# Layer norms of a graph network with the features on partitions, their product on GpSimd

## The chip, the cores and the metric

One core of a Trainium2 chip (trn2). The metric is the device time of one execution in microseconds. Each kernel ran several times; medians of all runs are quoted. All runs of this study are of the fast state. Ratios are computed as the mean time of one kernel's fast runs over that of the other's of the same rounds, so they are not quite the ratio of the medians quoted beside them.

## The reference

Sixteen graphs of 1024 nodes and 128 features share one sparse adjacency matrix (some 8 neighbours a node). Four layers follow each other: attention, graph attention (GAT), attention, attention. Only the end of each layer matters here:

```python
# attention layers (L0, L2, L3)
x1 = layer_norm(x + attn @ Wo + bo, ln1_g, ln1_b)
x  = layer_norm(x1 + relu(x1 @ W1 + b1) @ W2 + b2, ln2_g, ln2_b)
# graph attention layer (L1)
x  = layer_norm(x + attn, ln_gamma, ln_beta)

def layer_norm(x, g, b):       # over the 128 features
    mu, var = x.mean(-1, keepdims=True), x.var(-1, keepdims=True)
    return (x - mu) * rsqrt(var + 1e-5) * g + b
```

## The kernel before

The work is cut into 64 units (layer, half of the graphs, tile of 128 nodes) and each unit into parts. For each part GpSimd issues gathers of neighbour rows, VectorE makes the products, ScalarE the exponentials, TensorE the sums. What follows the sums of a unit, its **tail**, runs in two halves of four graphs each, interleaved with the next unit's parts: a tail is a generator, and `others()` advances all tails by about one step at each of three places in a part. Each engine works through its own instructions in program order; the timelines below show later ones waiting behind earlier ones.

```python
STEPS = 15            # steps of an attention unit's tails, spread evenly over the unit
GRAPH_STEPS = 8
...
def normed(y):                                   # y: nodes on partitions, PSUM
    z = twos.tile([P, GH, D], F32, tag="o", name="z")
    total = smalls.tile([P, GH], F32, tag="total", name="total")
    for i in range(GH):                          # GH = 4 graphs
        nc.scalar.activation(z[:, i, :], y[:, i, :], AF.Square, scale=D**-0.5, bias=root,
                             accum_out=total[:, i : i + 1])
    yield
    rstd = smalls.tile([P, GH], F32, tag="rstd", name="rstd")
    nc.gpsimd.tensor_tensor(rstd, total, power, ALU.pow)
    yield
    for i in range(GH):
        nc.scalar.activation(z[:, i, :], y[:, i, :], AF.Copy, scale=rstd[:, i : i + 1])
    return z

def turned(z, dst, gain=None, shift=None):       # transposes, then the eviction
    ps = bank([P, GH, P])
    for i in range(GH):
        nc.tensor.transpose(ps[:, i, :], z[:, i, :], ident)
    ...
        nc.scalar.activation(dst, ps, AF.Identity, bias=shift, scale=gain)

def attention_tail(l, g, t, h, o):
    ...
    for i in range(GH):                          # Wo, and x less its mean
        nc.tensor.matmul(ps[:, i, :], oT[:, i, :], p["Wo"], start=True, stop=False)
        nc.tensor.matmul(ps[:, i, :], xt[:, i, :], centre, start=False, stop=True)
    yield
    z = yield from normed(ps)
    yield
    x1 = twos.tile([P, GH, P], F32, tag="oT", name="x1")
    turned(z, x1, p["ln1_g"], p["ln1_b"])
    yield
    ...                                          # W1 and ReLU, then W2 + centre into ps
    z = yield from normed(ps)
    yield
    yield from finish(l, g, t, h, z, p["ln2_g"], p["ln2_b"])    # turned, next layer's projection

# the loop over parts, cut
    products(i)                                  # VectorE
    summed(i - 2)                                # TensorE
    others()
    exponentials(i)                              # VectorE reduce, ScalarE Exp
    others()
    weighted(i - 1, 0)                           # VectorE; frees the buffer of part i-1
    gathered(i - 1 + AHEAD)                      # GpSimd; waits for that buffer
    others()
```

Of the kernel before, what the change touches and what calls it, by code (L numbers as in the profile page):

```python
# [11 lines left out]

F32 = mybir.dt.float32
BF16 = mybir.dt.bfloat16
I32 = mybir.dt.int32
AF = mybir.ActivationFunctionType
ALU = mybir.AluOpType
# [3 lines left out]
P = 128  # L21
D = 128
# [3 lines left out]
F = FF // P  # L26
EPS = 1e-5
# [18 lines left out]
GH = G // HF  # L46
# [65 lines left out]
AHEAD = 4  # L112

LIMIT = 1e25


def rows_of(v, n=P):
# [5 lines left out]
def sparse_path(ctx: ExitStack, tc: tile.TileContext, a: dict, out: bass.AP, flag):  # L123


    nc = tc.nc
    const = ctx.enter_context(tc.tile_pool(name="const", bufs=1))
    dram = ctx.enter_context(tc.tile_pool(name="dram", bufs=1, space=DRAM))
    banks = ctx.enter_context(tc.tile_pool(name="banks", bufs=4, space=PSUM))
    ybanks = ctx.enter_context(tc.tile_pool(name="ybanks", bufs=2, space=PSUM))  # L130
    accs = ctx.enter_context(tc.tile_pool(name="accs", bufs=1, space=PSUM))

    def bank(shape):
        return banks.tile(shape, F32, tag="ps", name="ps")

    ident = const.tile([P, P], F32, name="ident")
    make_identity(nc, ident)

    centre = const.tile([P, P], F32, name="centre")
# [11 lines left out]
        q = slice(0, P) if whole else slice(32 * j, 32 * j + 32)  # L151
        return rep[q, j].rearrange("p s n -> p (s n)")

    power = const.tile([P, GH], F32, name="power")
    nc.vector.memset(power, -0.5)

    root = const.tile([P, 1], F32, name="root")
    nc.vector.memset(root, (EPS / D) ** 0.5)


    idx = const.tile([P, 2, T, J, QUADS], I32, name="idx")
# [8 lines left out]
    wts = ctx.enter_context(tc.tile_pool(name="wts", bufs=2))  # L170
    states = ctx.enter_context(tc.tile_pool(name="states", bufs=2))
# [4 lines left out]
    twos = ctx.enter_context(tc.tile_pool(name="twos", bufs=2))  # L176
# [260 lines left out]
    w = {}  # L437
# [12 lines left out]
    def load_weights(layer):  # L450



        t = wts.tile([P, 2 * D], F32, tag="Wkv", name="Wkv")
        nc.sync.dma_start(t[:, :D], a[f"{layer}_gnn_Wk"])
        nc.sync.dma_start(t[:, D:], a[f"{layer}_gnn_Wv"])
        w[layer, "Wkv"] = t
        yield
        for name in ATTN:
            src = a[f"{layer}_gnn_{name}"]  # L460
            if name in ("Wq", "Wo", "W1"):
                t = wts.tile([P, src.shape[1]], F32, tag=name, name=name)
                nc.sync.dma_start(t, src)
            elif name == "W2":
                t = wts.tile([P, F, D], F32, tag=name, name=name)
                nc.sync.dma_start(t, src.rearrange("(f p) d -> p f d", p=P))
            elif name == "b1":
                t = wts.tile([P, F], F32, tag=name, name=name)
                with nc.allow_non_contiguous_dma(reason="a bias, once"):
                    nc.sync.dma_start(t, src.rearrange("(f p) -> p f", p=P))  # L470
            elif name.startswith("ln") or name in ("b2", "bo"):
                t = wts.tile([P, 1], F32, tag=name, name=name)
                nc.sync.dma_start(t, src.rearrange("(p o) -> p o", o=1))
            else:
                continue
            w[layer, name] = t
        yield
        centred(w[layer, "Wo"], D)
        centred(w[layer, "W2"].rearrange("p f d -> p (f d)"), F * D)
        ps = bank([P, F])  # L480
        for f in range(F):
            nc.tensor.matmul(
                ps[:, f : f + 1], w[layer, "W1"][:, f * P : (f + 1) * P], w[layer, "b2"],
                start=True, stop=True,
            )
        nc.vector.tensor_tensor(w[layer, "b1"], w[layer, "b1"], ps, ALU.subtract)
        nc.vector.tensor_tensor(w[layer, "ln1_b"], w[layer, "ln1_b"], w[layer, "b2"], ALU.add)

    wg = const.tile([P, D + 2], F32, name="wg")

# [32 lines left out]
    xs = {}  # L523
# [48 lines left out]
        nc.sync.dma_start(table[:, h * GH * D : (h + 1) * GH * D], kv[:, : GH * D])  # L572
        nc.sync.dma_start(table[:, ROW + h * GH : ROW + (h + 1) * GH], kv[:, GH * D :])

    def normed(y):

        z = twos.tile([P, GH, D], F32, tag="o", name="z")
        total = smalls.tile([P, GH], F32, tag="total", name="total")
        for i in range(GH):
            nc.scalar.activation(  # L580
                z[:, i, :], y[:, i, :], AF.Square, scale=D**-0.5, bias=root,
                accum_out=total[:, i : i + 1],
            )
        yield
        rstd = smalls.tile([P, GH], F32, tag="rstd", name="rstd")
        nc.gpsimd.tensor_tensor(rstd, total, power, ALU.pow)  # L586
        yield
        for i in range(GH):
            nc.scalar.activation(z[:, i, :], y[:, i, :], AF.Copy, scale=rstd[:, i : i + 1])  # L589
        return z  # L590

    def turned(z, dst, gain=None, shift=None):
# [4 lines that stand above are left out]
        if gain is None:  # L597
            nc.scalar.copy(dst, ps)  # L598
        else:
            nc.scalar.activation(dst, ps, AF.Identity, bias=shift, scale=gain)  # L600

    def over_graphs(v):
        return v.rearrange("p (o d) -> p o d", o=1).to_broadcast([P, GH, D])

    def finish(l, g, t, h, z, gain, shift):
        if l + 1 < len(LAYERS):

            wanted[0] = True
            while held[0]:
                advance(slow)  # L610
            wanted[0] = False
            busy[0] += 1
            xn = states.tile([P, GH, P], F32, tag="xT", name="xT")
            turned(z, xn, gain, shift)
            yield
            yield from project(l + 1, g, t, h, xn)
            busy[0] -= 1
            return
        xn = states.tile([P, GH, P], F32, tag="xT", name="xT")
        turned(z, xn, gain, shift)  # L620
        yield
        o = twos.tile([P, GH, D], F32, tag="kv", name="outs")
        turned(xn, o)
        yield
        nc.gpsimd.indirect_dma_start(  # L625
            out=out.rearrange("n (k c) -> (n k) c", k=GR * HF),
            out_offset=bass.IndirectOffsetOnAxis(ap=places[:, g, h, t : t + 1], axis=0),
            in_=o.rearrange("p g d -> p (g d)"), in_offset=None,
        )

    def attention_tail(l, g, t, h, o):
        layer = LAYERS[l][0]
        p = {n: w[layer, n] for n in ATTN if (layer, n) in w}
        xt = xs[l, g, t][:, h]
        for _ in range(h):
            yield
        oT = twos.tile([P, GH, P], F32, tag="oT", name="oT")
        turned(o, oT)

        nc.scalar.activation(xt, xt, AF.Identity, bias=p["bo"])  # L640
        yield
        ps = ybanks.tile([P, GH, D], F32, tag="yps", name="yps")
        for i in range(GH):
            nc.tensor.matmul(ps[:, i, :], oT[:, i, :], p["Wo"], start=True, stop=False)  # L644
            nc.tensor.matmul(ps[:, i, :], xt[:, i, :], centre, start=False, stop=True)  # L645
        yield
        z = yield from normed(ps)
        yield
        x1 = twos.tile([P, GH, P], F32, tag="oT", name="x1")
        turned(z, x1, p["ln1_g"], p["ln1_b"])  # L650
        yield
        f1 = ones_.tile([P, F, GH * P], F32, tag="f1", name="f1")
        for f in range(F):
            ps = bank([P, GH * P])
            nc.tensor.matmul(  # L655
                ps, p["W1"][:, f * P : (f + 1) * P], x1.rearrange("p g n -> p (g n)"),
                start=True, stop=True,
            )
            nc.scalar.activation(f1[:, f, :], ps, AF.Relu, bias=p["b1"][:, f : f + 1])  # L659
        yield  # L660
        ps = ybanks.tile([P, GH, D], F32, tag="yps", name="yps")
        for i in range(GH):
            for f in range(F):
                nc.tensor.matmul(  # L664
                    ps[:, i, :], f1[:, f, i * P : (i + 1) * P], p["W2"][:, f, :],
                    start=(f == 0), stop=False,
                )
            nc.tensor.matmul(ps[:, i, :], x1[:, i, :], centre, start=False, stop=True)
        yield
        z = yield from normed(ps)  # L670
        yield
        yield from finish(l, g, t, h, z, p["ln2_g"], p["ln2_b"])

    def graph_tail(l, g, t, h, o):
        for _ in range(h):
            yield
        ps = ybanks.tile([P, GH, D], F32, tag="yps", name="yps")
        nc.tensor.matmul(
            ps.rearrange("p g d -> p (g d)"), ident, o.rearrange("p g d -> p (g d)"),
            start=True, stop=False,  # L680
        )
        for i in range(GH):
            nc.tensor.matmul(  # L683
                ps[:, i, :], xs[l, g, t][:, h, i, :], centre, start=False, stop=(i == GH - 1)
            )
        yield
        z = yield from normed(ps)
        yield
        yield from finish(l, g, t, h, z, w["L1", "ln_gamma"], w["L1", "ln_beta"])

    def natural(g, t, h, rows, kv=None):
# [325 lines left out]
    with tc.manual_schedule():  # L1017
# [37 lines left out]
        for i in range(len(parts) + 2):  # L1055
            here = i < len(parts)
            u = parts[i][0] if here else len(units)
            if here:
                l = units[u][0]
# [491 lines left out]
```

## Time and profile before

| | before |
|---|---|
| time, median (range) | 2544.95 us (2538.24 to 2557.18), 4 runs |
| busy: TensorE, VectorE, ScalarE, GpSimd | 82%, 75%, 58%, 57% |
| TensorE at half rate, after the first 250 us | 62 stretches, 357 us |
| VectorE waiting for gathers' transfers | 149 us |

The prediction below shows the waits, the stretches of one unit and the rows of the normalisation. Here, for comparison with later runs, are the rows of VectorE's two large products, from the groups of instructions by form; after the bar stand busy us, the mean in ns, and the idle time ahead of them with what ended it:

```profile
L919 DVE TENSOR_TENSOR pr<-e,ex 128x2048 f32<-128x2048 f32 x264 | 601.5, 2288 | 46.6 <-ACT ex L895 22.2 <-ACT ex L907 17.6 <-PE ps L596 3.7
L868 DVE TENSOR_TENSOR pr<-e,qr 128x2048 f32<-128x2048 f32 x198 | 453.4, 2290 | 177.8 <-PE acc L935 80.7 <-DMA e<-table,idx 70.6 <-ACT qr L831 16.8
```

A product of 128x2048 takes 2.29 us here in the mean. The runs below show what a longer mean comes from.

### The profile page before, as it was taken

To read this page: it belongs to the slowest core of one execution; us is meant where nothing else is said; L and a number is where in the kernel's file an instruction comes from. 1 tells how busy PE (TensorE), PEld (TensorE's weight loads), DVE (VectorE), ACT (ScalarE), POOL (GpSimd) and SP (SyncE) were. 2 spreads that over 40 slices of the span, in tenths; PEclk is the share of its full clock that TensorE was granted. 3 is DMA by queue.
4 is the path that set the end of the run, shared out by engine and by line. 5 is a ranking of instruction groups with operands and counts; after the bars stand their busy time and mean duration, and the time that the engine had idled before them with its cause. 6 is when DMAs were issued, how large, how long until landed. Compare 5 with 4: busy or idle time off the path is not lost. (4 is left out here: it accounts for less than half of the span.)

```text
span 2561.0 us, 36646 instructions
## 1 busy us (share of the span) xinstructions
PE 2102.6 (82%) x13124; PEld 1303.1 (51%) x13124; DVE 1930.3 (75%) x1470; ACT 1474.6 (58%) x4640; POOL 1450.8 (57%) x978
## 2 busy tenths in 40 slices
PE   6558989788887888988788888988888787888786
PEld 5425656445554554554455554555555454445454
DVE  7887787587877466667887879788797877787782
ACT  3216776565665444455476656667666665566555
POOL 3334666366666588784545545455555656665652
PEclk8679999899898999999899999999999898989888
DMA  7646888667678589898777877788777667567660
GB/s 251 232 170 230 293 280 287 210 227 252 231 257 260 175 282 327 281 322 297 276 256 248 298 258 261 255 283 277 264 267 254 222 240 260 203 222 257 222 222 24
DMA packets 168461, 636.05 MB, mean 248 GB/s; under 512 B 38328, under 2 KB 41144, under 8 KB 119774
## 3 DMA queue, kind: packets, MB, share of 16 engines
q0 software_dynamic: 92672, 485.09, 54.2%
q1 hardware_dynamic: 75600, 148.55, 17.4%
q8 instruction: 105, 1.72, 0.3%
q14 instruction: 84, 0.69, 0.1%
HBM read 603.11 MB, written 92.34 MB: 272 GB/s over the span
## 5 line engine op out<-in xcount | busy, mean ns | idle before, releaser
L856 POOL DMA_INDIRECT e<-table,idx x600 | 925.7, 1543 | 455.9 <-DVE pr L919 245.6
L919 DVE TENSOR_TENSOR pr<-e,ex 128x2048 f32<-128x2048 f32 (+1 forms) x336 | 689.5, 2060 | 205.0 <-ACT ex L895 174.2
L868 DVE TENSOR_TENSOR pr<-e,qr 128x2048 f32<-128x2048 f32 x204 | 460.7, 2258 | 177.8 <-PE acc L935 80.7
L586 POOL TENSOR_TENSOR rstd<-total,power 128x4 f32<-128x4 f32 x224 | 333.1, 1490 | 392.6 <-ACT z L580 385.4
L935 PE MATMUL acc<-pr,marks 128*32 128x512 f32 x2656 | 495.1, 618 | 38.2 <-DVE pr L919 38.2
L891 DVE TENSOR_REDUCE sc<-pr 128x128 f32<-128x2048 f32 (+1 forms) x252 | 518.5, 2058 | 8.6
L580 ACT ACTIVATE z<-yps,root 128x128 f32<-128x128 f32 x896 | 318.5, 378 | 98.5 <-PE yps L683 49.8
L596 PE MATMUL ps<-ident,z 128*128 128x128 f32 x896 | 212.7, 338 | 161.8 <-ACT z L589 161.7
L589 ACT ACTIVATE z<-yps,rstd 128x128 f32<-128x128 f32 x896 | 257.3, 381 | 102.4 <-POOL rstd L586 102.3
L596 PEld LDWEIGHTS ps<-ident,z 128*128 128x128 f32 x896 | 136.0, 159 | 345.4 <-ACT z L589 251.8
L659 ACT ACTIVATE f<-ps,b 128x512 f32<-128x512 f32 x192 | 131.9, 690 | 275.8 <-PE ps L655 275.8
L655 PE MATMUL ps<-x,W 128*128 128x512 f32 x384 | 249.1, 783 | 35.9 <-ACT x L600 35.8
L664 PE MATMUL yps<-W,f 128*128 128x128 f32 x1536 | 259.7, 287 | 17.0 <-ACT f L659 15.9
L664 PEld LDWEIGHTS yps<-W,f 128*128 128x128 f32 x1536 | 212.2, 196 | 77.5 <-ACT f L659 58.6
L935 PEld LDWEIGHTS acc<-pr,marks 128*32 128x32 f32 x2656 | 102.0, 112 | 283.8 <-issue 223.9
L538 PE MATMUL ps<-Wkv,xT 128*128 128x256 f32 x768 | 208.7, 416 | 32.7 <-ACT xT L600 24.1
L831 ACT COPY qr<-ps 128x512 f32<-128x512 f32 x384 | 197.0, 600 | 61.3 <-PE ps L828 55.7
L580 ACT ACTIVATION_READ_ACCUMULATOR z<-yps,root 128x1 f32 x896 | 194.1, 217 | 0.0
L542 ACT COPY kv<-ps 128x512 f32<-128x512 f32 x176 | 103.3, 589 | 140.9 <-PE ps L538 117.1
L538 PEld LDWEIGHTS ps<-Wkv,xT 128*128 128x128 f32 x768 | 146.4, 202 | 73.1 <-ACT xT L600 30.0
L644 PE MATMUL yps<-Wo,oT 128*128 128x128 f32 x768 | 160.9, 292 | 6.0 <-ACT oT L598 6.0
L645 PE MATMUL yps<-centre,x 128*128 128x128 f32 x768 | 158.0, 288 | 6.6
(159 smaller groups left out, 2663.6 us busy)
## 6 DMA issues: line engine op xcount, KB each, us to landing
table<-kv SPq DMA_DIRECT2D x88, 512.0 KB
qx<-qr SPq DMA_DIRECT2D x96, 256.0 KB
kept<-xT SPq DMA_DIRECT2D x96, 256.0 KB
x<-kept SPq DMA_DIRECT2D x48, 512.0 KB
e<-table,idx POOLq DMA_INDIRECT x600
table<-kv SPq DMA_DIRECT2D x32, 256.0 KB
edges<-in_adj SPq DMA_DIRECT2D x8, 512.0 KB
spare<-in_x SPq DMA_DIRECT2D x8, 512.0 KB
```

The costliest lines, as they stand in the source:

```text
L538: nc.tensor.matmul(ps[:, k, :], x[:, i + k, :], w[LAYERS[l][0], "Wkv"], start=True, stop=True,)
L580: nc.scalar.activation(z[:, i, :], y[:, i, :], AF.Square, scale=D**-0.5, bias=root, accum_out=total[:, i : i + 1],)
L586: nc.gpsimd.tensor_tensor(rstd, total, power, ALU.pow)
L589: nc.scalar.activation(z[:, i, :], y[:, i, :], AF.Copy, scale=rstd[:, i : i + 1])
L596: nc.tensor.transpose(ps[:, i, :], z[:, i, :], ident)
L655: nc.tensor.matmul(ps, p["W1"][:, f * P : (f + 1) * P], x1.rearrange("p g n -> p (g n)"), start=True, stop=True,)
L664: nc.tensor.matmul(ps[:, i, :], f1[:, f, i * P : (i + 1) * P], p["W2"][:, f, :], start=(f == 0), stop=False,)
L856: nc.gpsimd.indirect_dma_start(out=es[i][:, k, :], out_offset=None, in_=tables[l, g][:, :], in_offset=bass.IndirectOffsetOnAxis(ap=idx[:, ...
L868: nc.vector.tensor_tensor(prs[i][0][:, :n, :], es[i][:, :n, :ROW], qx[u].rearrange("p (o c) -> p o c", o=1) if (MIX, 0) in piece else of_p ...
L891: nc.vector.tensor_reduce(sc[:, :n, :], prs[i][0][:, :n, :].rearrange("p k (a d) -> p k a d", d=HD), mybir.AxisListType.X, ALU.add,)
L919: nc.vector.tensor_tensor(prs[i][k0 // 2][:, :m, :].rearrange("p k (a d) -> p k a d", d=d), es[i][:, k0 : k0 + m, base : base + ROW].rearr ...
L935: nc.tensor.matmul(outs[32 * j : 32 * j + 32], marks[:, mark, :], rhss, start=(r == 0 and chunk[0] != MIX), stop=(chunk == last),)
```

## The change

Its intent is to normalise without turning the data. Weights become the stationary operand, so `y` comes out of TensorE with the features on partitions and the nodes on the free axis, as the next matmul wants it. The mean of the squares over the partitions is then a matmul with a matrix of 1/128, which also copies it to all partitions. A node's deviation no longer is one scalar per partition, as the activation's scale was in the kernel before, so a product of two tensors takes its place. That goes to GpSimd. The gains and shifts of the first norm are folded into W1, b1, `centre` and two added vectors.

```diff
-    def normed(y):
-        ...                    # Squares with accumulators, power, Copies (above)
+    def normed(y, add=0.0):
+        squares = twos.tile([P, GH * P], F32, tag="oT", name="squares")
+        nc.scalar.activation(squares, y, AF.Square, bias=add)
+        z = twos.tile([P, GH * P], F32, tag="o", name="z")
+        nc.scalar.activation(z, y, AF.Identity, bias=add)
+        yield
+        ps = bank([P, GH * P])
+        nc.tensor.matmul(ps, ones.to_broadcast([P, P]), squares, start=True, stop=True)
+        yield
+        nc.scalar.activation(squares, ps, AF.Ln, bias=eps)
+        nc.scalar.activation(squares, squares, AF.Exp, scale=-0.5)
+        yield
+        nc.gpsimd.tensor_tensor(z, z, squares, ALU.mult)
         return z
...
     def finish(l, g, t, h, z, gain, shift):
-            turned(z, xn, gain, shift)
+            nc.scalar.activation(xn, z, AF.Identity, bias=shift, scale=gain)   # abridged
...
-        nc.scalar.activation(xt, xt, AF.Identity, bias=p["bo"])
-        for i in range(GH):
-            nc.tensor.matmul(ps[:, i, :], oT[:, i, :], p["Wo"], start=True, stop=False)
-            nc.tensor.matmul(ps[:, i, :], xt[:, i, :], centre, start=False, stop=True)
+        nc.tensor.matmul(y, p["Wo"], oT, start=True, stop=False)               # abridged
+        nc.tensor.matmul(y, centre, xt, start=False, stop=True)
+        x1 = yield from normed(y, w[layer, "add"][:, 0:1])                    # no turn
...                             # W1, ReLU as before, on x1
+        nc.tensor.matmul(y, w[layer, "centre"], x1, start=True, stop=False)
+        for f in range(F):
+            nc.tensor.matmul(y, p["W2"][:, f, :], f1[:, f, :], start=False, stop=(f == F - 1))
+        z = yield from normed(y, w[layer, "add"][:, 1:2])
+        yield from finish(...)                                                # no yield between
```

A load of the table set that holds Ln and Exp together is added at the start.

More of the change, by code (lines that the diff above doesn't have):

```diff
@@ L9 @@
 from concourse._compat import with_exitstack
+from concourse.hw_specs import get_activation_tables
 from concourse.bass_utils import run_bass_kernel_spmd
@@ L114 @@
 LIMIT = 1e25
+BOTH = list(get_activation_tables("gen3")).index("natural_log_exp_and_others")
 def rows_of(v, n=P):
@@ L152, in rep_of @@
         return rep[q, j].rearrange("p s n -> p (s n)")
-    power = const.tile([P, GH], F32, name="power")
-    nc.vector.memset(power, -0.5)
-    root = const.tile([P, 1], F32, name="root")
-    nc.vector.memset(root, (EPS / D) ** 0.5)
+    ones = const.tile([P, 1], F32, name="ones")
+    nc.vector.memset(ones, 1.0 / D)
+    eps = const.tile([P, 1], F32, name="eps")
+    nc.vector.memset(eps, EPS)
+    nc.scalar.add_instruction(
+        mybir.InstLoadActFuncSet(
+            name=nc.get_next_instruction_name(), act_func_set_id=BOTH,
+            engine=mybir.EngineType.Activation,
+        )
+    )
     idx = const.tile([P, 2, T, J, QUADS], I32, name="idx")
@@ L479, in load_weights @@
         centred(w[layer, "W2"].rearrange("p f d -> p (f d)"), F * D)
-        ps = bank([P, F])
+        ps = bank([P, F + 2])
         for f in range(F):
             nc.tensor.matmul(
-                ps[:, f : f + 1], w[layer, "W1"][:, f * P : (f + 1) * P], w[layer, "b2"],
+                ps[:, f : f + 1], w[layer, "W1"][:, f * P : (f + 1) * P], w[layer, "ln1_b"],
                 start=True, stop=True,
             )
-        nc.vector.tensor_tensor(w[layer, "b1"], w[layer, "b1"], ps, ALU.subtract)
         nc.vector.tensor_tensor(w[layer, "ln1_b"], w[layer, "ln1_b"], w[layer, "b2"], ALU.add)
+        for k, name in enumerate(("bo", "ln1_b")):
+            nc.tensor.matmul(
+                ps[:, F + k : F + k + 1], centre, w[layer, name], start=True, stop=True
+            )
+        nc.vector.tensor_tensor(w[layer, "b1"], w[layer, "b1"], ps[:, :F], ALU.add)
+        add = wts.tile([P, 2], F32, tag="add", name="add")
+        nc.vector.tensor_copy(add, ps[:, F:])
+        w[layer, "add"] = add
+        gain = w[layer, "ln1_g"]
+        nc.vector.tensor_scalar(w[layer, "W1"], w[layer, "W1"], gain, None, ALU.mult)
+        w[layer, "centre"] = wts.tile([P, P], F32, tag="centre", name="centre1")
+        nc.vector.tensor_scalar(w[layer, "centre"], centre, gain, None, ALU.mult)
     wg = const.tile([P, D + 2], F32, name="wg")
@@ L573, in project @@
         nc.sync.dma_start(table[:, ROW + h * GH : ROW + (h + 1) * GH], kv[:, GH * D :])
-    def normed(y):
-        z = twos.tile([P, GH, D], F32, tag="o", name="z")
-        total = smalls.tile([P, GH], F32, tag="total", name="total")
-        for i in range(GH):
-            nc.scalar.activation(
-                z[:, i, :], y[:, i, :], AF.Square, scale=D**-0.5, bias=root,
-                accum_out=total[:, i : i + 1],
-            )
+    def normed(y, add=0.0):
[3 more added lines that the diff above has]
+        nc.scalar.activation(z, y, AF.Identity, bias=add)
         yield
-        rstd = smalls.tile([P, GH], F32, tag="rstd", name="rstd")
-        nc.gpsimd.tensor_tensor(rstd, total, power, ALU.pow)
+        ps = bank([P, GH * P])
+        nc.tensor.matmul(ps, ones.to_broadcast([P, P]), squares, start=True, stop=True)
         yield
-        for i in range(GH):
-            nc.scalar.activation(z[:, i, :], y[:, i, :], AF.Copy, scale=rstd[:, i : i + 1])
+        nc.scalar.activation(squares, ps, AF.Ln, bias=eps)
+        nc.scalar.activation(squares, squares, AF.Exp, scale=-0.5)
+        yield
+        nc.gpsimd.tensor_tensor(z, z, squares, ALU.mult)
         return z
@@ L600, in turned, with scaled @@
             nc.scalar.activation(dst, ps, AF.Identity, bias=shift, scale=gain)
-    def over_graphs(v):
-        return v.rearrange("p (o d) -> p o d", o=1).to_broadcast([P, GH, D])
     def finish(l, g, t, h, z, gain, shift):
+        def scaled():
+            xn = states.tile([P, GH, P], F32, tag="xT", name="xT")
+            nc.scalar.activation(
+                xn.rearrange("p g n -> p (g n)"), z, AF.Identity, bias=shift, scale=gain
+            )
+            return xn
         if l + 1 < len(LAYERS):
@@ L612, in finish @@
             busy[0] += 1
-            xn = states.tile([P, GH, P], F32, tag="xT", name="xT")
-            turned(z, xn, gain, shift)
+            xn = scaled()
             yield
@@ L618, in finish @@
             return
-        xn = states.tile([P, GH, P], F32, tag="xT", name="xT")
-        turned(z, xn, gain, shift)
+        xn = scaled()
         yield
@@ L638, in attention_tail @@
         turned(o, oT)
-        nc.scalar.activation(xt, xt, AF.Identity, bias=p["bo"])
         yield
-        ps = ybanks.tile([P, GH, D], F32, tag="yps", name="yps")
-        for i in range(GH):
-            nc.tensor.matmul(ps[:, i, :], oT[:, i, :], p["Wo"], start=True, stop=False)
-            nc.tensor.matmul(ps[:, i, :], xt[:, i, :], centre, start=False, stop=True)
+        y = ybanks.tile([P, GH * P], F32, tag="yps", name="yps")
+        nc.tensor.matmul(
+            y, p["Wo"], oT.rearrange("p g n -> p (g n)"), start=True, stop=False
+        )
+        nc.tensor.matmul(
+            y, centre, xt.rearrange("p g n -> p (g n)"), start=False, stop=True
+        )
         yield
-        z = yield from normed(ps)
-        yield
-        x1 = twos.tile([P, GH, P], F32, tag="oT", name="x1")
-        turned(z, x1, p["ln1_g"], p["ln1_b"])
+        x1 = yield from normed(y, w[layer, "add"][:, 0:1])
         yield
@@ L655, in attention_tail @@
             nc.tensor.matmul(
-                ps, p["W1"][:, f * P : (f + 1) * P], x1.rearrange("p g n -> p (g n)"),
-                start=True, stop=True,
+                ps, p["W1"][:, f * P : (f + 1) * P], x1, start=True, stop=True
             )
@@ L660, in attention_tail @@
         yield
-        ps = ybanks.tile([P, GH, D], F32, tag="yps", name="yps")
-        for i in range(GH):
-            for f in range(F):
-                nc.tensor.matmul(
-                    ps[:, i, :], f1[:, f, i * P : (i + 1) * P], p["W2"][:, f, :],
-                    start=(f == 0), stop=False,
-                )
-            nc.tensor.matmul(ps[:, i, :], x1[:, i, :], centre, start=False, stop=True)
+        y = ybanks.tile([P, GH * P], F32, tag="yps", name="yps")
+        nc.tensor.matmul(y, w[layer, "centre"], x1, start=True, stop=False)
+        for f in range(F):
+            nc.tensor.matmul(
+                y, p["W2"][:, f, :], f1[:, f, :], start=False, stop=(f == F - 1)
+            )
         yield
-        z = yield from normed(ps)
-        yield
+        z = yield from normed(y, w[layer, "add"][:, 1:2])
         yield from finish(l, g, t, h, z, p["ln2_g"], p["ln2_b"])
@@ L676, in graph_tail @@
             yield
-        ps = ybanks.tile([P, GH, D], F32, tag="yps", name="yps")
+        y = ybanks.tile([P, GH * P], F32, tag="yps", name="yps")
         nc.tensor.matmul(
-            ps.rearrange("p g d -> p (g d)"), ident, o.rearrange("p g d -> p (g d)"),
-            start=True, stop=False,
+            y, centre, xs[l, g, t][:, h].rearrange("p g n -> p (g n)"), start=True, stop=False
         )
@@ L683, in graph_tail @@
             nc.tensor.matmul(
-                ps[:, i, :], xs[l, g, t][:, h, i, :], centre, start=False, stop=(i == GH - 1)
+                y[:, i * P : (i + 1) * P], o[:, i, :], ident, start=False, stop=(i == GH - 1)
             )
         yield
-        z = yield from normed(ps)
-        yield
+        z = yield from normed(y)
         yield from finish(l, g, t, h, z, w["L1", "ln_gamma"], w["L1", "ln_beta"])
```

## The prediction

> **What bounds the kernel now.** I first read the busy shares on the page.
>
> ```profile
> PE 2102.6 (82%) x13124; PEld 1303.1 (51%) x13124; DVE 1930.3 (75%) x1470; ACT 1474.6 (58%) x4640; POOL 1450.8 (57%) x978
> ```
>
> No engine is full. The chain that ended last covers only the final 4 us here, so it settles nothing. I then read the waits (engine, line, whom it waited for: us in total, times, longest us):
>
> ```profile
> POOL rstd L586 <- ACT z L580: 385.4, 110, 12.7
> ACT f L659 <- PE ps L655: 275.8, 176, 5.5
> ...
> DVE pr L919 <- ACT ex L895: 174.2, 58, 10.9
> PE ps L596 <- ACT z L589: 161.7, 79, 7.7
> ...
> ACT z L589 <- POOL rstd L586: 102.3, 61, 7.6
> ```
>
> TensorE waits for the normalised rows before it transposes them (L596), ScalarE waits for TensorE before each ReLU (L659), and VectorE, which does the heavy products, waits for ScalarE's exponentials (L919). It is a ring of in-order engines. One of its turns, by stretches of 2 us (columns: stretch, length, busy us of PE, PEld, DVE, ACT, POOL, then granted clock, DMA share, GB/s):
>
> ```profile
> 1462.00:1464.00 2.00, 0.76 (x8) 0.00 (x0) 2.00 (x2) 2.00 (x9) 1.28 (x2) 1.00 0.94 343
> 1464.00:1466.00 2.00, 1.21 (x4) 0.55 (x4) 1.97 (x3) 1.67 (x9) 1.30 (x2) 0.89 1.00 393
> 1466.00:1468.00 2.00, 1.23 (x2) 0.71 (x3) 2.00 (x2) 1.75 (x5) 1.70 (x2) 0.50 0.94 344
> 1468.00:1470.00 2.00, 2.00 (x3) 0.69 (x3) 2.00 (x2) 0.69 (x1) 2.00 (x1) 0.50 0.89 340
> 1470.00:1472.00 2.00, 2.00 (x7) 0.84 (x7) 1.97 (x2) 1.24 (x2) 1.70 (x2) 0.50 0.87 250
> 1472.00:1474.00 2.00, 2.00 (x11) 0.63 (x7) 1.77 (x1) 0.22 (x1) 1.31 (x2) 0.90 0.98 401
> 1474.00:1476.00 2.00, 2.00 (x20) 2.00 (x19) 0.00 (x0) 0.00 (x0) 0.00 (x0) 1.00 0.98 377
> 1476.00:1478.00 2.00, 2.00 (x10) 1.03 (x8) 0.00 (x0) 0.48 (x1) 0.00 (x0) 1.00 1.00 369
> ```
>
> First TensorE starves while a normalisation runs on ScalarE and GpSimd. Then its clock drops to 0.50. Then it works off a backlog at 1474 to 1478 while VectorE, ScalarE and GpSimd stand still. VectorE's gap lasts 5.5 us, and the pattern returns about once per unit (one layer, graph group and 128-node tile; some 40 us). In the trace's clock records after 250 us there are 62 half-rate stretches, 357 us together. In 54 of them the largest TensorE gap in the 3.4 us before is one that ends with an L596 transpose. So the normalisation chain is my bottleneck, through TensorE's starving and backlog.
>
> **What the Trainium skill says.**
> - "TensorE: Matmul & The Clock Gate", Part 1 (the HAM clock gate): TensorE runs at half rate after idle windows of about 3.4 us. The trace agrees in kind (0.50 above), though about 2 us of pure idling with little work around it was enough.
> - "SBUF — State Buffer", Who interferes with whom: a VectorE instruction with two SBUF inputs excludes a GpSimd instruction that reads SBUF; whichever starts first blocks the other. The trace agrees in one direction: the powers (L586) that began during a large VectorE product took 2.05 us (85 of them), those that began with VectorE idle 1.03 us (74). The products are hardly delayed (2.30 against 2.29 us), as a power reads only 4 elements per partition.
> - "GPSIMD Engine Reference", §3.1: a two-input elementwise operation costs about 2.6 cycles per element at 1.2 GHz. For 512 elements that is an estimated 1.1 us plus overhead. No row before has this shape.
> - "ScalarE: Activation LUTs", Table sets: one set holds both exp and ln. So Ln should bring no table switches; no run here shows it yet, but the built program has one table load, as before.
>
> **The change, part by part.** There are 224 normalisations, two in each of 96 attention tails and one in each of 32 graph tails. These are the rows that go or shrink (busy us, mean ns, then idle before them):
>
> ```profile
> L586 POOL TENSOR_TENSOR rstd<-total,power 128x4 f32<-128x4 f32 x224 | 333.1, 1490 | 392.6 <-ACT z L580 385.4
> L580 ACT ACTIVATE z<-yps,root 128x128 f32<-128x128 f32 x896 | 318.5, 378 | 98.5 <-PE yps L683 49.8
> L596 PE MATMUL ps<-ident,z 128*128 128x128 f32 x896 | 212.7, 338 | 161.8 <-ACT z L589 161.7
> L589 ACT ACTIVATE z<-yps,rstd 128x128 f32<-128x128 f32 x896 | 257.3, 381 | 102.4 <-POOL rstd L586 102.3
> L659 ACT ACTIVATE f<-ps,b 128x512 f32<-128x512 f32 x192 | 131.9, 690 | 275.8 <-PE ps L655 275.8
> ```
>
> *ScalarE.* In the timeline four Squares with their accumulator reads take 1.40 us, four Copies 1.16 us, and the scaled eviction of the transposes 0.78 us: 3.34 us. An attention tail adds 0.73 us for the bias on its input (L640). In their place come four 128x512 activations, at 0.69 us each (the ReLU row) less a little overlap: 2.6 us; only a final normalisation (128 of 224) keeps 0.78 us of scaling. Attention tail: 2×3.34+0.73 = 7.4 becomes 2×2.6+0.78 = 6.0, saving 1.4 us × 96 = 138 us. Graph tail: 3.34 becomes 3.38, nothing.
>
> *TensorE.* From starts in the timeline at full clock, a 128-column matmul costs 0.223 us (12 in 2.68 us), a 512-column one 0.853, four transposes 0.44. Attention tail before: 20 small matmuls and 8 transposes, 4.46+0.88 = 5.34 us. After: 2 for Wo, 3 for W2 and 2 for the means of squares, 7×0.853 = 5.97. That is 0.63 more, × 96 = 60 us. Graph tail about 0.37 more, × 32 = 12 us. So TensorE's work *rises* by 72 us at full clock, since the means cost more than the transposes they replace. Fewer weight loads gain nothing by themselves: they are already hidden.
>
> *GpSimd.* The power of 1.49 us mean becomes a product of 128x512: estimated 1.4 us alone, 1.9 with blocking; 224 × 0.4 = some 90 us more busy.
>
> *VectorE.* Same work, but now the GpSimd product reads long enough to hold it off. By the phases in which powers began (a third of the time VectorE idle, a quarter in its reduce, the rest in a product) I estimate 0.45 us per product: 224 × 0.45 = 100 us.
>
> *The chain of one normalisation.* Before: Squares 1.40, power 1.0 (more with blocking), Copies 1.16, transposes 0.5, eviction 0.78: 4.8 us. After: Square 0.69, means 0.85, Ln and Exp 1.3, product 1.4 (+0.78 where it feeds the next layer): 4.2 or 5.0 us. Its length stays. What changes is that TensorE gets a matmul in the middle of it, after just one activation, and waits at its end for GpSimd rather than ScalarE. Also the second accumulation now starts with the `centre` matmul, which needs no ReLU, so TensorE can begin the backlog earlier.
>
> *The sum.* TensorE +72, perhaps half exposed: +35. VectorE's hold-offs +100, half exposed as it is some 80% busy in the attention layers: +45. ScalarE −138, a third on the path through the exponentials: −45. Half-rate stretches cost up to 357/2 = 178 us; if a third of that goes with the transposes' waits: −60. Together −25: about **2530 us**. The exposed shares are my judgement.
>
> **Rivals.**
> 1. *The starving ends.* TensorE is kept warm by the means, so VectorE's gap of 5.5 us per unit mostly goes. For it: 54 of 62 half-rate stretches follow waits of L596, which disappear. Against: W1 and the projections now wait for GpSimd. Halving 48 such gaps gives −130 us: about 2430.
> 2. *GpSimd takes the wait over.* The product queues behind gathers in GpSimd's order and behind VectorE's products, and ScalarE's last scaling stands directly behind it in the same step. For it: the powers already stretched to 3.2 us, and gathers wait 246 us for VectorE. Against: a tail has several parts' slack. Time: 2620 to 2680.
> 3. *TensorE's load decides.* +72 us fully exposed with the same half-rate stretches: about 2620.
>
> **Range and chances.** The terms are each 50 to 100 us and of opposite sign, so 2440 to 2640 should hold it 8 times in 10. The 2% limits are about 2500 and 2602. I give 0.35 faster, 0.42 the same, 0.23 slower.
>
> **What the new profile would show.** Right: no L596 transposes of z; means x448 (two instructions per matmul) near 0.85 us a pair at full clock; four activations near 0.65 us each; GpSimd product 1.7 to 2.2 us mean; some VectorE products over 2.6 us; half-rate stretches a third fewer; ScalarE about 138 us less busy. Wrong: TensorE's largest wait is for GpSimd's product (rival 2), or half-rate stretches nearly gone (rival 1), or VectorE's products stretched by far more than 0.45 us per normalisation. A wrong share of exposure would break the time even if every duration holds.

## The result, and the profile after

The changed kernel is correct and slower: 2662.28 us median (2656.09 to 2682.59, 4 runs) against 2544.95, ratio 1.047 (95% interval 1.040 to 1.054). That is outside the predicted range of 2440 to 2640.

The busy shares of the changed kernel, from its page, to be held against the first line in the prediction:

```profile
PE 2114.4 (80%) x9808; PEld 984.3 (37%) x9808; DVE 2013.6 (76%) x1479; ACT 1332.9 (50%) x2656; POOL 1540.5 (58%) x978
```

ScalarE is 142 us less busy (138 predicted), GpSimd 90 us more (90 predicted), TensorE hardly changed. VectorE has nearly the same instructions and is 83 us busier. So the parts were sized well, and no engine is more than a point nearer to full. The waits tell more (engine, line, whom it waited for: us in total, times, longest us):

```profile
ACT f L678 <- PE ps L675: 345.5, 150, 8.7
POOL z L609 <- issue: 325.9, 80, 7.7
ACT xT L625 <- POOL z L609: 302.9, 119, 6.7
...
PEld ps L675 <- POOL z L609: 195.6, 82, 8.0
...
DVE pr L933 <- ACT ex L909: 139.8, 48, 8.6
```

L609 is GpSimd's product. (The second line is GpSimd's own idle time ahead of it; more on it below.) ScalarE's scaling (L625) waits 303 us for it, and TensorE's W1 (L675) waits 128 us with its matmuls and 196 us with its weight loads, which largely cover the same times. The ReLU behind W1 waits 346 us, against 276 before. The transposes' wait of 162 us is gone; this took its place. The groups of instructions by form:

```profile
L933 DVE TENSOR_TENSOR pr<-e,ex 128x2048 f32<-128x2048 f32 x264 | 630.1, 2396 | 59.7 <-ACT ex L921 44.9 <-ACT ex L909 14.1 <-PE acc L949 0.6
...
L609 POOL TENSOR_TENSOR z<-z,squares 128x512 f32<-128x512 f32 x224 | 347.9, 1553 | 460.2 <-issue 325.9 <-ACT squares L607 71.8 <-ACT ex L921 49.4
L604 PE MATMUL ps<-squares,ones 128*128 128x512 f32 x448 | 242.7, 628 | 26.3 <-ACT qr L845 25.6 <-ACT squares L599 0.8
...
L606 ACT ACTIVATE squares<-ps,eps 128x512 f32<-128x512 f32 x224 | 154.6, 690 | 31.7 <-PE ps L604 30.0
```

The means (two overlapping instructions of 0.63 us each), Ln (0.69 us) and Exp (0.63 us) are about as long as predicted; the trace holds one table load, at the start, as before. The product takes 1.55 us in the mean, less than the 1.9 estimated. But VectorE's product is at 2.40 us where it was 2.29. How one such wait comes about can be read in the timeline (start, length, engine, line, operation, idle before it):

```profile
1509.42 3.11 POOL L870 DMA_INDIRECT e<-table,idx  x1 [0.30 <-PE ps L675]
...
1511.59 2.28 DVE L882 TENSOR_TENSOR pr<-e,qr 128x2048 f32<-128x2048 f32 x1
1512.56 2.44 POOL L609 TENSOR_TENSOR z<-z,squares 128x512 f32<-128x512 f32 x1
...
1515.05 3.53 PE L675 MATMUL ps<-z,W 128*128 128x512 f32 x4 [3.30 <-POOL z L609]
...
1517.23 0.69 ACT L678 ACTIVATE f<-ps,b 128x512 f32<-128x512 f32 x1 [7.33 <-PE ps L675]
...
1519.49 1.23 DVE L933 TENSOR_TENSOR pr<-e,ex 128x1024 f32<-128x1024 f32 x1 [3.29 <-ACT ex L909]
```

The second half's product should follow its Exp, which ends at 1506.95, but two gathers stand ahead of it in GpSimd's queue, the last one taking 3.1 us. At 1512.56 it starts, in the middle of a VectorE product of two SBUF inputs that runs until 1513.87; it ends 1.13 us after that, so it was held. Only then do TensorE (idle 3.30 us, now at half rate: four instructions take 3.53 us) and the ReLU (ScalarE idle 7.33 us) go on. The exponential that VectorE needs stands behind the ReLU, so VectorE idles 3.29 us. The opposite order occurs as well:

```profile
1523.90 1.27 POOL L609 TENSOR_TENSOR z<-z,squares 128x512 f32<-128x512 f32 x1 [6.42 <-issue]
1523.91 3.40 DVE L882 TENSOR_TENSOR pr<-e,qr 128x2048 f32<-128x2048 f32 x1 [3.19 <-PE acc L949]
```

GpSimd begins 10 ns earlier, and VectorE's product takes 3.40 us, 1.1 more than usual. In the mean, VectorE's products of 128x2048 that begin during a GpSimd product take 3.12 us (47 of them), the others 2.32.

Over the trace, from the end of Exp to the start of the product 2.0 us pass in the mean and over 5.7 us in one case of ten. But in half of the cases it is GpSimd that waits: 115 of the 224 products start within 0.4 us of their Exp. GpSimd is idle for 460 us in all just before its products, and 457 us of that end so, though the profile names no releaser for 326 us (`issue`; the 6.42 us above are such a case). While it stands there, the gathers that come next in its queue aren't issued. It stood before its powers in the same way, for 393 us, in the kernel before.

### The profile page after: what moved, and what is told of

It reads as the page before. It is cut to its first block, busy times and chain, and to the rows that moved or that the text cites. A ratio compares the mean times of both kernels' runs of the same rounds, so it can differ in the third digit from the quotient of the medians.

```text
span 2657.9 us, 28115 instructions
## 1 busy us (share of the span) xinstructions
PE 2114.4 (80%) x9808; PEld 984.3 (37%) x9808; DVE 2013.6 (76%) x1479; ACT 1332.9 (50%) x2656; POOL 1540.5 (58%) x978
## 5 line engine op out<-in xcount | busy, mean ns | idle before, releaser
L609 POOL TENSOR_TENSOR z<-z,squares 128x512 f32<-128x512 f32 x224 | 347.9, 1553 | 460.2 <-issue 325.9
L675 PE MATMUL ps<-z,W 128*128 128x512 f32 x384 | 207.2, 666 | 128.2 <-POOL z L609 127.8
L604 PE MATMUL ps<-squares,ones 128*128 128x512 f32 x448 | 242.7, 628 | 26.3 <-ACT qr L845 25.6
L683 PE MATMUL yps<-f,W 128*128 128x512 f32 x384 | 180.8, 593 | 0.0
L625 ACT ACTIVATE xT<-z,ln_b,ln_g 128x512 f32<-128x512 f32 x96 | 78.0, 813 | 203.5 <-POOL z L609 203.2
L606 ACT ACTIVATE squares<-ps,eps 128x512 f32<-128x512 f32 x224 | 154.6, 690 | 31.7 <-PE ps L604 30.0
L675 PEld LDWEIGHTS ps<-z,W 128*128 128x128 f32 x384 | 70.3, 200 | 249.6 <-POOL z L609 195.6
L842 PE MATMUL ps<-q,rep 32*128 32x512 f32 x768 | 143.8, 669 | 13.9 <-ACT q L837 13.2
L599 ACT ACTIVATE squares<-yps,add 128x512 f32<-128x512 f32 x192 | 133.2, 694 | 32.5 <-PE yps L683 29.1
L607 ACT ACTIVATE squares<-squares 128x512 f32<-128x512 f32 x224 | 141.2, 630 | 7.1
L989 DVE TENSOR_TENSOR o<-acc,both 128x512 f32<-128x512 f32 x128 | 85.3, 689 | 66.5 <-ACT xT L625 59.5
```

Of the source, the lines that this page charges most:

```text
L604: nc.tensor.matmul(ps, ones.to_broadcast([P, P]), squares, start=True, stop=True)
L606: nc.scalar.activation(squares, ps, AF.Ln, bias=eps)
L609: nc.gpsimd.tensor_tensor(z, z, squares, ALU.mult)
L675: nc.tensor.matmul(ps, p["W1"][:, f * P : (f + 1) * P], x1, start=True, stop=True)
L683: nc.tensor.matmul(y, p["W2"][:, f, :], f1[:, f, :], start=False, stop=(f == F - 1))
```

## The experiments

The theory, **A**: the product on GpSimd is the loss, by its place in the chain, its occupation of GpSimd and its exclusion of VectorE. The rivals: **B**, the exclusion of VectorE alone, and **C**, the added TensorE work for the means. Fifteen kernels ran, each timed in 3 rounds against the kernel before on the same chip. As they ran on several chips, I compare runs of different calls by their ratios to the kernel before; 1% is some 25 us.

| run | median us | ratio to before (95%) |
|---|---|---|
| changed kernel | 2662 | 1.047 (1.040 to 1.054) |
| e1, no product (wrong result) | 2351 | 0.922 (0.920 to 0.924) |
| e10, product unread (wrong result) | 2508 | 0.982 (0.976 to 0.988) |
| e11, fills in its place (wrong result) | 2463 | 0.962 (0.956 to 0.967) |
| e9, gathers after the steps | 2613 | 1.021 (1.013 to 1.029) |
| e5, a step before the scaling | 2639 | 1.035 (1.029 to 1.040) |
| e2, product on VectorE | 2607 | 1.023 (1.020 to 1.026) |
| e7, e13, e14: one, two, three steps later | 2524, 2540, 2550 | 0.990, 0.998, 1.002 |
| e3, before + idle product | 2643 | 1.036 (1.033 to 1.039) |
| e8, before + idle fills | 2771 | 1.087 (1.082 to 1.092) |
| e4, before + idle matmul | 2583 | 1.014 (1.010 to 1.018) |
| e6, before with Ln and Exp | 2486 | 0.977 (0.971 to 0.982) |
| e12, e15: that in one step | 2616, 2737 | 1.022, 1.077 |

### e1: without the product

```diff
-        nc.scalar.activation(z, y, AF.Identity, bias=add)
+        nc.scalar.activation(z, y, AF.Identity, bias=add, scale=0.9)
...
-        nc.gpsimd.tensor_tensor(z, z, squares, ALU.mult)
```

> The changed kernel without the GpSimd product: z is scaled by the constant 0.9 inside its Identity activation and goes straight on (wrong result on purpose; Square, means, Ln and Exp still run, nobody reads them). Theory A, the product's place in the chain and its exclusion of VectorE are the loss: the 117 us come back and the waits for L609 vanish, 2480 to 2560 us. Rival C, the 72 us of TensorE work for the means is the loss: little changes, 2620 to 2660 us.

Measured: 2351 us, even faster than expected. The product costs 12.5% (1.047 less 0.922), some 318 us, and the rest of the change is worth −7.8%, some 198 us. This run also frees W1 and the scaling from waiting for Exp, but that is hardly part of it: in 95 of 96 attention tails W1 starts after that Exp's end all the same, 2.7 us after it in the median. C falls: the means run here as well. The waits show GpSimd left with little but gathers, which wait for their buffers:

```profile
POOL e L869 <- DVE pr L932: 678.8, 185, 21.8
...
ACT f L677 <- PE ps L674: 199.2, 62, 6.6
```

VectorE's wait for exponentials is at 82 us, where it was 174 before the change, and half-rate stretches after 250 us fall from 357 to 184 us.

### e4: the matmul alone

```diff
         nc.gpsimd.tensor_tensor(rstd, total, power, ALU.pow)
+        extra = bank([P, GH * P])
+        nc.tensor.matmul(extra, ident, rep.rearrange("p j s n -> p (j s n)"), start=True, stop=True)
```

> The kernel before with one 128x512 matmul on constant inputs added per normalisation, unread: 224 x 0.853 = 191 us more TensorE work at full clock, where the change added a net 72. Rival C: 2620 to 2720 us. Theory A: the extra work falls into TensorE's starving and may even keep its clock up, 2530 to 2590 us.

Measured: 2583 us, +1.4%, within what A expects. An estimated 191 us of TensorE work at full clock cost 35 us, so if the cost goes with the work, the change's net 72 are worth an estimated 13. Half-rate stretches fell from 357 to 160 us, with TensorE busy 86% of the span where it was 82%.

### e3 and e8: exclusion or occupation, in the kernel before

The tile `junk` is allocated once at the start, which the cut leaves out.

```diff
         nc.gpsimd.tensor_tensor(rstd, total, power, ALU.pow)
+        full = rep.rearrange("p j s n -> p (j s n)")                 # e3
+        nc.gpsimd.tensor_tensor(junk, full, full, ALU.mult)          # e3
+        for _ in range(4):                                           # e8
+            nc.gpsimd.memset(junk, 1.0)                              # e8
```

> The kernel before with one 128x512 GpSimd product added after each power; its inputs are constant and nobody reads its result, so it is on no chain, but it occupies GpSimd and excludes VectorE as in the changed kernel. If the exclusion (rival B) is the loss: VectorE's large products again about 0.1 us longer in the mean, 2600 to 2660 us. If the loss is that others wait for the product (theory A): 2545 to 2590 us.

Measured: 2643 us, +3.6%. VectorE's products grew as in the changed kernel:

```profile
L923 DVE TENSOR_TENSOR pr<-e,ex 128x2048 f32<-128x2048 f32 x264 | 629.4, 2394 | 44.8 <-ACT ex L899 28.4 <-ACT ex L911 14.0 <-PE ps L600 0.9
```

By its expectation this spoke for B. The fills, which only write, were to test that:

> The kernel before with four unread fills of 128x512 bf16 on GpSimd after each power: they occupy GpSimd for an estimated 1.2 to 2 us, as the idle product did for 1.4, but read nothing from SBUF. If the 95 us that the idle product cost came from excluding VectorE's two-input products: VectorE's products back at 2.29 us and 2545 to 2580 us. If they came from GpSimd being occupied (gathers and powers later): 2620 to 2680 us.

Measured: 2771 us, +8.7%, above both ranges, with fills of 0.52 us each, so 2.1 us at a time against 1.4. VectorE was not held off at all:

```profile
L923 DVE TENSOR_TENSOR pr<-e,ex 128x2048 f32<-128x2048 f32 x264 | 601.0, 2286 | 54.3 <-ACT ex L899 30.9 <-ACT ex L911 16.8 <-issue 3.3
```

So exclusion isn't needed for the loss; occupying GpSimd suffices. In the kernel before, though, GpSimd's queue also holds the powers, on which ScalarE waits (102 us before):

```profile
ACT z L593 <- POOL rstd L588: 263.7, 119, 7.1
```

The two runs therefore mix the delay of gathers with that of powers. The split had to be made where no power is.

### e10 and e11: the product's 12.5% taken apart

Both start from e1. In e10 the product runs at its old place on its old inputs, unread; in e11 fills of the same total length stand there.

```diff
+        nc.gpsimd.tensor_tensor(squares, z, squares, ALU.mult)       # e10
+        for _ in range(3):                                           # e11
+            nc.gpsimd.memset(squares, 1.0)                           # e11
```

> The run without the product (2351 us), with the GpSimd product issued in its old place on its old inputs, but its result goes back into the squares and nobody reads it (wrong result on purpose). It splits the 311 us: what it costs above 2351 us is the occupation of GpSimd (gathers behind it) and the hold-off of VectorE; what is missing to 2662 us is the waiting for its result. If waiting is most of it (rival 2 of the prediction): 2400 to 2480 us. If occupation and hold-off are most of it: 2550 to 2640 us.

> As the unread product, but with three fills of the squares (128x512, estimated 1.6 us together, writing only) in its place. VectorE's products should be back at 2.29 us. If hold-off of VectorE is what the unread product costs above 2351 us, this run is at 2350 to 2380 us; if it is GpSimd's occupation, this run is as slow as the unread product or slower.

Measured: 0.982 and 0.962. From e1 to the fills it is 3.9%, some 101 us: **occupation** of GpSimd's queue. From there to the unread product, which is about as long in all (368 us against 354), 2.1%, some 53 us: mostly **holding off** VectorE. From there to the changed kernel, where others need the result, 6.5%, some 164 us: **waiting**. The intervals leave each of the three uncertain by some 15 to 25 us. The unread product lay between the two ranges expected, and the fills met neither of theirs: no share is nearly all.

The three shares are not pure. The fills write the tile that Exp writes, so GpSimd also stands in its queue until Exp is done:

```profile
POOL squares L610 <- ACT squares L607: 288.1, 88, 10.6
```

Occupation is thus 354 us of work and 288 us of standing, with gathers behind both; no run here separates the two. The unread product is read by nobody, but it holds its buffers, and others wait 51 us for these, VectorE alone 30 (5 us in all for the fills). And VectorE is 49 us busier in e10 than in e11 but 82 us busier in the changed kernel, so some holding off lies in the last share too. VectorE's products show which run holds it off, e10 first, then e11:

```profile
L933 DVE TENSOR_TENSOR pr<-e,ex 128x2048 f32<-128x2048 f32 x264 | 617.9, 2350 | 21.6 <-ACT ex L909 15.5 <-ACT ex L921 5.3 <-PE acc L949 0.6
```

```profile
L934 DVE TENSOR_TENSOR pr<-e,ex 128x2048 f32<-128x2048 f32 x264 | 602.7, 2293 | 29.3 <-ACT ex L910 21.6 <-ACT ex L922 6.4 <-PE acc L950 0.6
```

Where occupation costs shows in VectorE's waits for the gathers' transfers, first e1, then e11:

```profile
DVE sc L913 <- DMA e<-table,idx: 73.8, 32, 4.9
DVE pr L881 <- DMA e<-table,idx: 71.0, 31, 9.5
```

```profile
DVE pr L883 <- DMA e<-table,idx: 111.8, 41, 9.0
DVE sc L915 <- DMA e<-table,idx: 101.0, 42, 5.1
```

145 us became 213, which fits gathers that go out later. In the changed kernel this wait is only 92 us, perhaps as VectorE is late itself there; so the shares hold only for this order of taking the product apart.

### e9: gathers behind the products

```diff
                 weighted(i - 1, 0)
-                gathered(i - 1 + AHEAD)
             others()
...
             others()
+            if 0 < i <= len(parts):
+                gathered(i - 1 + AHEAD)
```

> The changed kernel with each part's gather issued after that part's last step of the tails and not ahead of it, so that a product of that step no longer stands behind a gather that waits for VectorE to free its buffer. If the queue behind gathers is most of the waiting: waits for L609 fall by a third or more, 2550 to 2620 us. If it is only moved to the next step's products: 2640 to 2690 us.

Measured: 2613 us, 2.6% below the changed kernel. Now 170 of 224 products start within 0.4 us of their Exp, where it was 115. The wait of the scaling fell by a third, those of W1 from 128 to 85 and from 196 to 122 us. So the queue behind gathers is a real part of the waiting. But what the products gained, the gathers lost; VectorE's wait for their transfers in the attention layers rose from 39 us in the changed kernel to 222:

```profile
DVE pr L882 <- DMA e<-table,idx: 221.8, 76, 9.2
...
ACT xT L625 <- POOL z L609: 205.6, 114, 6.8
```

### e5: one more step ahead of the scaling

```diff
-STEPS, GRAPH_STEPS = 15, 8
+STEPS, GRAPH_STEPS = 16, 9
         nc.gpsimd.tensor_tensor(z, z, squares, ALU.mult)
+        if apart:             # at the end of a tail
+            yield
```

> The changed kernel with one more step between the GpSimd product and the scaling that reads it at the end of a tail (steps per unit 15 to 16 and 8 to 9), so ScalarE does not stand directly behind the product. If that missing step is what makes the waits costly: waits of the scaling for the product fall from 303 to under 120 us and the time to 2540 to 2600 us. If the queue and the exclusion matter wherever the consumer stands: 2620 to 2680 us.

Measured: 2639 us, in the second range. The scaling's wait did vanish (303 to 44 us), but W1's grew (128 to 184 us) and the ReLU's with it (346 to 402 us). Removing one wait for the product handed most of the time to the next one.

### e2, e7, e13, e14: the product on VectorE

```diff
-        nc.scalar.activation(z, y, AF.Identity, bias=add)
...
         nc.scalar.activation(squares, squares, AF.Exp, scale=-0.5)
         yield                                      # e7, e13, e14: 1, 2, 3 more yields
-        nc.gpsimd.tensor_tensor(z, z, squares, ALU.mult)
+        nc.vector.scalar_tensor_tensor(z, y, add, squares, ALU.add, ALU.mult)
```

STEPS and GRAPH_STEPS are raised to 17 and 9, 19 and 10, 21 and 11 in the three later ones.

> The changed kernel with the product on VectorE, as (y + add) * rstd with y read from PSUM, so the Identity activation goes too (ScalarE about 150 us less busy, VectorE about 224 x 0.69 = 155 us more, less some 85 us of hold-offs). Theory A (waiting for GpSimd behind gathers): 2500 to 2580 us, waits of W1 and of the scaling under 100 us each. If VectorE's load decides instead: 2640 to 2720 us. Rival C: 2640 to 2700 us.

Measured: 2607 us, 2.4% better than on GpSimd but between the ranges. GpSimd's waits are gone; a new one took their place, as VectorE's queue is in order as well:

```profile
DVE z L608 <- ACT squares L605: 430.6, 153, 12.9
```

> The run with the product on VectorE out of PSUM, with one more step between Exp and the product (steps 17 and 9), as there VectorE stood 431 us waiting for Exp. If that in-order wait is what cost it: the wait under 150 us, 2420 to 2540 us. If the 155 us of added VectorE work decide: 2580 to 2620 us.

Measured: 2524 us, which beats the kernel before by 1%. The wait is shorter, though not under 150 us:

```profile
DVE z L609 <- ACT squares L605: 312.4, 94, 13.7
```

> The product on VectorE out of PSUM, two steps later than at first (steps 19 and 10). If VectorE's in-order wait for Exp is the cost: that wait falls from 312 to 200 us or less and the time to 2420 to 2490 us. If the 155 us of VectorE work are: 2510 to 2550 us.

> As that, three steps later (steps 21 and 11). In-order wait: 2400 to 2470 us, unless the tails, which now need 21 steps in a unit, end too late; then slower than with two steps. Work: 2510 to 2560 us.

Measured: 2540 and 2550 us, in the ranges expected of the added work. But neither did what was expected of the in-order wait: it stayed, at 340 us with two steps and 338 with three. More steps in the same unit follow each other more closely: the product starts 0.50, 0.59 and 0.59 us after its Exp in the median with one, two and three steps. So these runs did not test the wait, and how much of VectorE's cost is the wait and how much the added work stays open.

### e6, e12, e15: one part of the change, in the kernel before

```diff
-        nc.gpsimd.tensor_tensor(rstd, total, power, ALU.pow)
+        nc.scalar.activation(rstd, total, AF.Ln)
+        nc.scalar.activation(rstd, rstd, AF.Exp, scale=-0.5)
```

The load of the common table set is added as well.

> The kernel before with one part of the change alone: the deviation by Ln and Exp on ScalarE (two activations of 128x4) in the place of the power on GpSimd; layout, transposes and steps as before. If GpSimd's place in the chain costs the kernel before as well: 2400 to 2500 us, waits of L589 for the deviation gone and half-rate stretches under 357 us. If only the 512-wide product is harmful: 2530 to 2570 us.

Measured: 2486 us, 2.3% faster than the kernel before (interval of the ratio 0.971 to 0.982), correct: the best version of this study, in the range that says GpSimd's place in the chain cost the kernel before too. ScalarE's wait for the power is gone, and half-rate stretches fell from 357 to 298 us; the transposes' waits fell from 162 to 95 us (matmuls) and from 253 to 170 (weight loads), and GpSimd, which no longer stands before powers, reaches its gathers early. VectorE's wait for transfers fell from 149 to 99 us, and the gathers now wait for their buffers:

```profile
POOL e L866 <- DVE pr L929: 762.8, 183, 21.8
...
PEld ps L606 <- ACT z L599: 170.1, 89, 3.2
```

e12 then put Squares, Ln, Exp and Copies into one step (two yields less per normalisation, steps 11 and 6), and e15 did so at the old steps of 15 and 8.

> The kernel before with Ln and Exp for the power (2486 us) and, as all of the normalisation is then on ScalarE, Squares, Ln, Exp and Copies in one step (steps 15 to 11 and 8 to 6). If the latency of the normalisation's steps is still what starves TensorE: 2400 to 2470 us. If the longer stretch on ScalarE holds up the exponentials instead: 2490 to 2540 us.

> The one-step normalisation by Ln and Exp (2616 us) at the old pace (steps 15 and 8 again, of which the tails use 11 and 6, so they end early). If the slower pace made it slow: 2420 to 2500 us. If the longer stretch on ScalarE did: 2570 to 2630 us.

Measured: 2616 and 2737 us, both slower than e6, and each above both of its ranges. The slower pace was not the reason, since the old pace made it worse. In e15 VectorE waits far longer for the exponentials (166 us in e6), as one expects of the longer stretch on ScalarE:

```profile
DVE pr L927 <- ACT ex L903: 374.4, 106, 11.3
```

In e12 that wait is 172 us, hardly more than in e6, so its loss has another cause, which stays open.

## Why the prediction was wrong, point by point

- *ScalarE −138 us, GpSimd +90 us, VectorE's hold-offs +45 us of time.* Right in size: −142 and +90 us of busy time, VectorE 83 us busier (100 estimated). What it costs in time is not cleanly measured: from e11 to e10 it is some 53 us, with waits for buffers in it.
- *TensorE +72 us, half exposed.* Too much: e4, scaled down, puts all of it at about 13 us.
- *Half-rate stretches a third fewer.* 357 became 285 us, a fifth. The reading behind it was too wide as well: L596 also transposes attention outputs and gathered rows, which stay. Of the 54 stretches put down to it, some 47 follow transposes of z in a recount.
- *"Its length stays" and "a tail has several parts' slack".* These are the steps that failed. I counted the product at 1.4 us and compared sums of durations. Its duration was about right. But it stands in an in-order queue behind gathers and is held by VectorE's products, so it starts 2.0 us after Exp in the mean, in one case of ten over 5.7, and in-order engines stand behind it. That waiting costs some 164 us; the sum had nothing for it. The prediction's own sign of being wrong came true: TensorE's largest waits are for GpSimd's product (128 and 196 us). Nor did I count what occupying GpSimd's queue costs everything behind it, some 101 us from e1 to the fills: I put 90 us on GpSimd's busy time and left them out of the sum. The power cost something there too, so not all of the 101 are new; taking it away gained 2.3% (e6), with Ln and Exp paid for.
- *The sum.* Its −25 gives 2520 us from the 2545 measured, not 2530; nothing hangs on that. Without the product it was +35 −45 −60 = −70 us; e1 shows −198. The product was +45; it costs 318. Two terms were mis-sized in opposite directions, and the larger was on the side of the loss. Of the 198, some 59 may be the power's leaving GpSimd, as in e6; that the two add up was not tested.
- *The rivals.* Rival 2, "GpSimd takes the wait over", named the mechanism and the place, with 2620 to 2680 us. I gave it too little weight. Rival 1 is what the layout does once the product is away (e1). Rival 3 falls with e4.

## What to carry to other kernels

When a step moves to another engine, ask first what stands ahead of it in that engine's queue, what it will itself wait for there, and who waits for its result; the engine's busy share says nothing on these. GpSimd was 57% busy, and unread fills on it (354 us, and 288 us of standing until they could start) still cost some 101 us, with the gathers that feed everything else in the same queue. A layout that needs one more product of two tensors is only worth what the engine left for it can take: here the layout gained 7.8% and the product cost 12.5%, while the small half of the idea, Ln and Exp on ScalarE in the place of a power on GpSimd, gained 2.3% by itself.

## What the Trainium skill lacked or had wrong

- "SBUF — State Buffer", Who interferes with whom, says that a VectorE instruction with two SBUF inputs contends with a GpSimd instruction that reads SBUF, but not with one that only writes it. The fills agree (VectorE's products stay at 2.286 us in e8). How long the one holds the other it says for VectorE's two-port modes, not for two inputs. The 128x512 product holds about as long as it runs (VectorE 3.40 instead of 2.28 us, against a product of 1.27 us). The power of 128x4 does not: it takes 1.0 us, yet VectorE's products that began during one took 2.30 us against 2.29. It is as if the hold lasted only as long as the reading, which no run here separates.
- "GPSIMD Engine Reference", §3.1, gives about 2.6 cycles per element for two inputs, which at 1.2 GHz makes an estimated 1.11 us for 512 elements. Measured 1.28 us in the median, some 0.17 us more. It has no figure for a power; here 1.04 us in the median for 4 elements.
- No page says what work on GpSimd costs gathers queued there. A gather holds GpSimd 1.4 to 1.7 us here (mean of 600), and 354 us of unrelated fills between them, which also stood 288 us for their own tile, made VectorE wait 68 us longer for their transfers and the kernel some 101 us slower.
